# Where GpSimd makes the sums of Wf in a two-layer graph kernel

## The chip, the cores and the metric

One core of one Trainium2 chip runs the kernel. The metric is the device time of a launch in microseconds (us); the time before is the median of three runs. TensorE is PE in the profile, its weight loads are PEld, VectorE is DVE, ScalarE is ACT, GpSimd is POOL, and SP is the engine whose queue issues the DMAs.

## The reference, cut to what matters

The input is `x`, 128 graphs of 64 nodes with 768 features, and `adj`, a mask of 64 x 64 for each graph. Both layers have the form `x = layernorm(x + layer(x, adj))`. Layer 0 is a graph attention with 12 heads, a gate and an ELU. Layer 1, in which the change lies, is a masked attention with six heads of 128:

```
q, k, v = heads(x @ Wq + bq), heads(x @ Wk + bk), heads(x @ Wv + bv)
scores  = einsum('bhqd,bhkd->bhqk', q, k) / sqrt(128)
probs   = softmax(scores + (0 where adj, else -9e15))
ctx     = einsum('bhqk,bhkd->bhqd', probs, v)
x       = layernorm(x + ctx @ Wf + bf)
```

Everything is float32.

## The kernel before, in words

The 8192 tokens are 64 tiles of 128 rows. A pair is two tiles, a group is two pairs. Phase A computes layer 0 pair by pair, and also the products with Wv, whose results go to `v_d` in DRAM. Phase B computes the rest of layer 1 group by group, 16 groups in all.

**Products by sums.** Phase B's products with Wq, Wk and Wf are done by a scheme that needs 15 block products where the plain way needs 18. The token side is split into 6 blocks and the weight into 9; further operands are sums or differences of blocks. The list `SUMS` has the eleven of the token side (`S` for q and k, `Sc` for the context), the list `WEIGHT_SUMS` the fourteen of a weight. `STEPS` lists the 15 block products, each with its token operand, its weight slot, its accumulator and the outputs that it goes to. Each is one step of a `Stream`: four TensorE matmuls in the profile (L896). Each result is added to its outputs by ACT and DVE (L917, L922, L939).

**Who makes the sums.** `weight15_sum(wb, k, eng, o)` makes sum `k` of the weight in tile `wb` on engine `eng` over the columns `o`. On one line (L167) it makes the sums of Wq and Wk, in two halves of the columns (the first half on DVE, the second on POOL), and those of Wf, whole and all on POOL. In the profile the weights have the name `w` whichever they are; a whole sum is 128x512. The token sums of group 0 are made early on DVE, all later ones on POOL by `sum_of_group` (L285). Group 1's are each due two steps after the step of group 0's last stream that reads the tile they overwrite. The first four of group 0's have tiles of their own, so the same sums of group 1 have no such reader. The sums of the context tiles are `pair_sum` (L878).

**What sets the order.** The program is written in steps. `at(step, f)` puts a piece of work on the list of a step, and `run` goes through the lists in order; each engine gets its instructions in the order in which they are so issued, and runs them in that order. The tile framework adds the waits on semaphores. A step of a product comes ahead of all else on its list. Group `g` begins at step `90 * g`: four streams of 15 steps for q and k, of which the last two belong to the odd heads. The following 30 steps hold the two products with Wf of the group before; in group 0 they are empty of products, so on TensorE group 1's first step (step 90) comes right behind step 59 and the group's last scores (L961).

**The softmax of a group** lies in the steps of the next one. For group 0 it starts at step 95, with four parts (`q`, `i`) four steps apart. For a part it is: maximum (`sm_top`, L979, DVE), subtraction (`sm_sub`, L998, DVE), exponential (`sm_exp`, L1001, ACT) three steps after the maximum, row sum (`sm_total`, L1005, DVE), reciprocal and scaling (`sm_scale`: L1009 on DVE, then L1010 on POOL) seven steps after the maximum, transposes on TensorE (`probs`, L1016) with a copy by ACT (L1022) ten steps after it, and the context matmuls (`context`, L1036) thirteen steps after it. The first transposes thus stand at step 105, on TensorE's queue among the steps of group 1's products.

**The sums of Wf.** The tile `wf` takes the place of the weight Wv, which phase A has used up; its six loads stand at steps 2 to 7 (L156), its first sum at step 8, and POOL's halves of the sums of Wq and Wk at steps 9 to 34. The thirteen other sums of Wf stand at steps 68 to 92, two steps apart. Between them and step 34, POOL has group 1's eleven token sums, at steps 47 to 59; after them comes the first scaling of group 0's softmax, at step 102. The first product with Wf is at step 150.

Of the kernel before, what the change touches and what calls it, by code (L numbers as in the profile page):

```python
# [61 lines left out]
def kernel(  # L62
# [31 lines left out]
    nc = tc.nc  # L94
# [52 lines left out]
    def weight15(i):  # L147
        return wts.tile([P, 7, CH, HALF], F32, name=f"w{i}", tag=f"w{i}").rearrange(
            "p s c o -> p (s c o)"
        )[:, : 15 * 2 * 256].rearrange("p (s c o) -> p s c o", s=15, c=2)  # L150
# [14 lines left out]
    def weight15_sum(wb, k, eng, o=slice(0, 256)):  # L165
        to, a, b, sign = WEIGHT_SUMS[k]
        eng.tensor_tensor(wb[:, to, :, o], wb[:, a, :, o], wb[:, b, :, o], SIGN[sign])  # L167
# [647 lines left out]
    def phase_b(ctx, wq, wk, early_sums):  # L815
# [272 lines left out]
        def at(step, *fs):  # L1088
            events.setdefault(max(step, 0), []).extend(fs)
# [14 lines left out]
        wf = weight15(2)  # L1104
# [7 lines left out]
            for k in range(len(WEIGHT_SUMS)):  # L1112
                at(9 + 12 * n + k, lambda wb=wb, k=k: weight15_sum(wb, k, nc.gpsimd, slice(P, 2 * P)))
        for k in range(1, len(WEIGHT_SUMS)):
            at(66 + 2 * k, lambda k=k: weight15_sum(wf, k, nc.gpsimd))
        for g in range(NG):
            d, o = st[g], N * g
            d["S"] = {} if g else early_sums
# [98 lines left out]
    with tc.manual_schedule():  # L1217
        with ExitStack() as c:
            early = phase_a(c)
        with ExitStack() as c:  # L1220
            phase_b(c, *early)
# [31 lines left out]
```

## The time and the profile before

| | |
|---|---|
| median of three runs | 2874.41 us (2872.54 to 2874.44) |
| the profiled execution's own time | 2871.92 us |
| its span | 2870.1 us |
| granted TensorE clock, mean | 0.997 |
| PE busy | 2823.4 us (98%) |
| PEld busy | 2062.7 us (72%) |
| DVE busy | 1862.2 us (65%) |
| POOL busy | 1546.7 us (54%) |
| ACT busy | 1200.4 us (42%) |
| PE's share of the chain that ended last | 85% |

The span is the part of the profiled execution from its first instruction to its last; the time of an execution is 1.8 us more. All times of single events below are microseconds from the span's start. Phase B's first products start at about 1464 us.

A line of a timeline holds the start, the time taken, the engine, the line in the code, the operation with its output and inputs, the count, and in brackets the idle time before it with what ended it. A row of the view of stretches holds the stretch, its length, the busy time and count of PE, PEld, DVE, ACT and POOL, then the granted TensorE clock (1.00 is full), the share of the DMA engines and GB/s.

### The profile page before, as it was taken

How to read it: one execution, taken by the hardware profiler on the slowest of the kernel's cores; microseconds unless marked ns; L12 is line 12 of the kernel's file. 1: busy time of each engine (PE TensorE's matmuls, PEld its weight loads, DVE VectorE, ACT ScalarE, POOL GpSimd, SP SyncE). 2: the span in 40 equal slices, each digit the busy share in tenths (PEclk: the TensorE clock that was granted, in tenths of full speed). 3: DMA queues.
4: the chain of work that ended last, by engine and by line, in shares of the span. 5: the costliest groups of instructions: out<-in, count | busy, mean ns of one | idle time of the engine just before them, and what ended most of it. 6: DMA issues, size and time to landing. Idle time of an engine off the chain costs nothing.

```text
span 2870.1 us, 50797 instructions
## 1 busy us (share of the span) xinstructions
PE 2823.4 (98%) x18108; PEld 2062.7 (72%) x18108; DVE 1862.2 (65%) x3724; ACT 1200.4 (42%) x3737; POOL 1546.7 (54%) x1653
## 2 busy tenths in 40 slices
PE   8899999999999999999999999999999999999998
PEld 5556666555565665655577888888888888888887
DVE  4887777777877777778664555555555555555556
ACT  4666656566566565665622221222221222211223
POOL 4755555555555565555545545345555446454455
PEclk9999999999999999999999999999999999999999
DMA  5434445445344454453631221212221212211222
GB/s 167 121 113 138 147 125 144 128 134 151 114 140 146 126 144 128 134 149 115 210 134 34 89 74 60 79 58 88 90 70 59 83 57 90 89 64 59 89 83 73
DMA packets 358684, 308.40 MB, mean 107 GB/s; under 512 B 226592, under 2 KB 304160, under 8 KB 358432
## 3 DMA queue, kind: packets, MB, share of 16 engines
q1 hardware_dynamic: 358432, 305.16, 34.7%
q8 instruction: 144, 2.36, 0.3%
q14 instruction: 108, 0.88, 0.1%
HBM read 191.41 MB, written 101.06 MB: 102 GB/s over the span
## 4 chain that ended last, share of the span: by engine, by line
PE 85%; DVE 6%; POOL 3%; DMA 2%; ACT 2%; issue 1%; SPq 1%; DVEq 0%; POOLq 0%; ACTq 0%
PE X L896 42%; PE X L209 36%; PE pb L1036 2%; PE pb L961 2%; PE pa L603 1%; DMA s<-dst_d 1%; PE pa L585 1%; PE pb L1016 1%; DVE z L645 1%; ACT s L548 1%; POOL w L167 1%; ACT s L564 1%; DVE s L555 1%; DVE z L636 1%; DVE w L173 0%
## 5 line engine op out<-in xcount | busy, mean ns | idle before, releaser
L209 PE MATMUL X<-w,S 128*128 128x384 f32 x2304 | 796.1, 490 | 10.6 <-DVE w L173 3.3
L896 PE MATMUL X<-S,w 128*128 128x256 f32 x2752 | 651.3, 382 | 0.0
L209 PEld LDWEIGHTS X<-w,S 128*128 128x128 f32 x2304 | 429.9, 190 | 298.0 <-DVE w L173 5.2
L209 PE MATMUL X<-w,T 128*128 128x384 f32 x1728 | 598.1, 489 | 6.9 <-ACT snap L434 5.0
L896 PEld LDWEIGHTS X<-S,w 128*128 128x128 f32 x2752 | 513.6, 190 | 70.1
L209 PEld LDWEIGHTS X<-w,T 128*128 128x128 f32 x1728 | 325.5, 191 | 233.7 <-ACT snap L434 16.2
L878 POOL TENSOR_TENSOR Sc<-cT 128x256 f32<-128x256 f32 x224 | 162.4, 731 | 404.3 <-PE X L896 401.7
L896 PE MATMUL X<-w,Sc 128*128 128x256 f32 x1408 | 322.5, 381 | 0.9 <-DVE xs L939 0.8
L939 DVE TENSOR_TENSOR xs<-xs,X 128x256 f32<-128x256 f32 x512 | 210.6, 419 | 169.0 <-PE X L896 160.5
L896 PEld LDWEIGHTS X<-w,Sc 128*128 128x128 f32 x1408 | 265.5, 190 | 38.5 <-DVE xs L939 1.6
L564 ACT ACTIVATE s<-s,nmx 128x64 f32<-128x64 f32 x768 | 256.2, 335 | 76.7 <-DVE nmx L559 76.7
L922 DVE TENSOR_TENSOR k<-k,X 128x256 f32<-128x256 f32 x320 | 133.5, 421 | 229.2 <-PE X L896 177.3
L896 PE MATMUL X<-xb,w 128*128 128x256 f32 x1024 | 253.1, 380 | 0.4 <-ACT q L917 0.4
L922 DVE TENSOR_TENSOR q<-q,X 128x256 f32<-128x256 f32 x320 | 133.2, 420 | 179.3 <-PE X L896 146.8
L321 ACT ACTIVATE xs<-xs,shift,rstd 128x768 f32<-128x768 f32 x62 | 63.5, 1024 | 417.5 <-POOL shift L317 409.0
L434 ACT COPY snap<-X 128x384 f32<-128x384 f32 x288 | 135.5, 470 | 229.5 <-PE X L209 227.1
L917 ACT ACTIVATE k<-X,bk_c 128x256 f32<-128x256 f32 x192 | 91.1, 474 | 306.3 <-PE X L896 306.3
L498 POOL TENSOR_TENSOR tmp<-th,wd_bc 128x768 f32<-128x768 f32 x64 | 147.5, 2305 | 130.5 <-ACT th L494 107.6
L896 PEld LDWEIGHTS X<-xb,w 128*128 128x128 f32 x1024 | 193.7, 190 | 26.9 <-ACT q L917 0.8
L917 ACT ACTIVATE q<-X,bq_c 128x256 f32<-128x256 f32 x192 | 91.0, 474 | 275.3 <-PE X L896 275.3
L548 ACT ACTIVATE s<-s,src 128x64 f32<-128x64 f32 x768 | 193.1, 335 | 30.5 <-DMA s<-dst_d 30.5
L312 POOL TENSOR_TENSOR rstd<-rstd,neg_half 128x1 f32<-128x1 f32 x126 | 69.4, 551 | 235.0 <-DVE rstd L311 233.7
(120 smaller groups left out, 4103.5 us busy)
## 6 DMA issues: line engine op xcount, KB each, us to landing
xb<-in_x_dram SPq DMA_DIRECT2D x64, 384.0 KB
s<-dst_d SPq DMA_DIRECT2D x128, 192.0 KB
x_d<-xb SPq DMA_DIRECT2D x64, 384.0 KB
xT_d<-T SPq DMA_DIRECT2D x64, 384.0 KB
v_d<-v SPq DMA_DIRECT2D x128, 192.0 KB
xb<-xT_d SPq DMA_DIRECT2D x32, 768.0 KB
xb<-v_d SPq DMA_DIRECT2D x256, 96.0 KB
xs<-x_d SPq DMA_DIRECT2D x64, 384.0 KB
```

The costliest lines, as they stand in the source:

```text
L209: nc.tensor.matmul(o, self.lhsT(i, c), rhs, start=first and c == 0, stop=last and c == CH - 1, skip_group_check=True,)
L312: nc.gpsimd.tensor_tensor(rstd, rstd, neg_half, ALU.pow)
L321: nc.scalar.activation(r, r, AF.Identity, bias=shift, scale=rstd)
L434: nc.scalar.copy(t, ps)
L498: nc.gpsimd.tensor_tensor(self.tmp, self.th, wd_bc, ALU.mult)
L548: nc.scalar.activation(self.s[:, a], self.s[:, a], AF.Prelu, bias=self.src[:, a : a + 1], alpha=LEAKY_ALPHA,)
L564: nc.scalar.activation(self.s[:, a], self.s[:, a], AF.Exp, bias=self.nmx[:, a : a + 1], accum_out=self.sm[:, a : a + 1],)
L878: nc.gpsimd.tensor_tensor(t, pair_part(d, q, r0), pair_part(d, q, r1), op)
L896: nc.tensor.matmul(ps, self.lhsT(r, slot, c), self.rhs(r, slot, c), start=start and c == 0, stop=stop and c == 1, skip_group_check=True,)
L917: nc.scalar.activation(o[:, b], ps, AF.Identity, bias=bias[:, hd : hd + 1], scale=1.0 if positive else -1.0)
L922: nc.vector.tensor_tensor(o[:, b], o[:, b], ps, ALU.add if positive else ALU.subtract)
L939: nc.vector.tensor_tensor(o, o, ps, ALU.add if positive else ALU.subtract)
```

## The change

The thirteen sums of Wf behind the first get other steps. Numbers 1 to 7 go to steps 36 to 42, behind the halves of Wq and Wk (step 34) and in front of group 1's token sums (step 47). Numbers 8 to 13 go to step 66, behind those token sums (step 59) and in front of the first scaling (step 102). Their order among themselves stays. No other work is moved.

```diff
         for k in range(1, len(WEIGHT_SUMS)):
-            at(66 + 2 * k, lambda k=k: weight15_sum(wf, k, nc.gpsimd))
+
+            at(35 + k if k < 8 else 66, lambda k=k: weight15_sum(wf, k, nc.gpsimd))
```

The empty line that comes with it moves the later lines of the code down by one.

## The prediction

> **What bounds the kernel now.** I read the page's busy shares first: PE is busy for 2823.4 of 2870.1 us, so only PE's gaps, or slow matmuls, can give anything. Then the view of waits for PE from 1464 us, the start of layer 1, to the end:
>
> ```profile
> PE pb L1016 <- POOL s L1010: 6.9, 1, 6.9
> PE X L896 <- DVE xs L939: 0.8, 1, 0.8
> PE X L896 <- ACT q L917: 0.4, 1, 0.4
> ```
>
> There is one real wait (us, times, longest): the first transposes of group 0's softmax (L1016) wait 6.9 us for POOL to scale the probabilities (L1010). The timeline of POOL says why:
>
> ```profile
> 1474.48 22.61 POOL L167 TENSOR_TENSOR w<-w 128x512 f32<-128x512 f32 x29 [20.68 <-DMA w<-in_L_gnn_Wf_dram]
> 1497.05 2.50 POOL L285 TENSOR_TENSOR S<-xb 128x512 f32<-128x512 f32 x2
> 1509.69 1.27 POOL L285 TENSOR_TENSOR S<-xb 128x512 f32<-128x512 f32 x1 [10.14 <-PE X L896]
> 1512.28 2.49 POOL L285 TENSOR_TENSOR S<-xb 128x512 f32<-128x512 f32 x2 [1.32 <-PE X L896]
> ...
> 1521.23 1.28 POOL L285 TENSOR_TENSOR S<-xb,S 128x512 f32<-128x512 f32 x1
> 1522.46 17.54 POOL L167 TENSOR_TENSOR w<-w 128x512 f32<-128x512 f32 x13
> 1539.95 1.62 POOL L1010 TENSOR_TENSOR s<-s,rs 128x384 f32<-128x384 f32 x2
> ```
>
> POOL makes two of group 1's token sums at 1497.05, then idles 10.14 us, because the next one overwrites a tile that group 0's matmuls still read. It finishes the eleven at 1522.5, and only then makes thirteen sums of Wf in one block. The scaling is queued behind that block, though its input was there earlier, as the timeline of DVE shows:
>
> ```profile
> 1532.13 0.18 DVE L1009 RECIPROCAL rs<-sm 128x6 f32<-128x6 f32 x1
> ```
>
> On PE's timeline the wait has a second cost:
>
> ```profile
> 1532.89 1.03 PE L896 MATMUL X<-S,w 128*128 128x256 f32 x4
> 1540.84 0.90 PE L1016 MATMUL pb<-ident,s 128*128 128x128 f32 x3 [6.92 <-POOL s L1010]
> 1541.53 1.91 PE L896 MATMUL X<-S,w 128*128 128x256 f32 x4
> 1543.24 1.50 PE L896 MATMUL X<-xb,w 128*128 128x256 f32 x4
> ```
>
> Four matmuls that take 1.03 us ahead of the gap take 1.91 and 1.50 after it. The view of stretches has the clock (the last three columns are PEclk, DMA share, GB/s):
>
> ```profile
> 1533.90:1540.80 6.90, 0.01 (x1) 0.00 (x0) 1.72 (x3) 0.47 (x1) 6.67 (x7) 0.75 0.00 0
> ...
> 1543.00:1544.00 1.00, 1.00 (x4) 0.82 (x3) 0.00 (x0) 0.52 (x2) 0.00 (x0) 0.50 0.00 0
> 1544.00:1545.00 1.00, 1.00 (x5) 0.81 (x5) 0.16 (x1) 0.37 (x1) 0.00 (x0) 0.91 0.00 0
> ```
>
> The clock is at 0.50 from about the middle of the gap to about 1544.2. What this costs is read against group 1, where the same three transposes and three steps run without a wait. From the chain of waits, group 1:
>
> ```profile
> 1629.41 0.33 PE pb L1016 x3
> 1629.74 2.59 PE X L896 x12
> 1632.33 0.86 PE pb L1036 x48
> ```
>
> In group 1 it is 1632.33 - 1629.41 = 2.92 us from the transposes to the context matmuls (L1036). In group 0 the contexts start at 1545.60 in the same view, 4.76 us after 1540.84. From there both groups keep one pace: 4.84 us from one context to the next.
>
> **What the Trainium skill says.** "TensorE: Matmul & The Clock Gate", Part 1, What's actually happening: after an idle window of about 3.4 us PE falls to half clock, and sustained work of about the same length brings it back. The trace agrees: 0.50, and back some 3.4 us after 1540.84. "SBUF — State Buffer", SBUF: two separate sides: a DVE operation with two SBUF inputs and a GpSimd operation that reads SBUF lock each other out for a whole instruction. The trace agrees: DVE's L998 (inputs s and mx) takes up to 1.54 us beside POOL's sums, against a median of 0.55, while L922, with one input in PSUM, has 418 ns beside a busy POOL (1475 to 1497) and 421 where POOL mostly idles (1497 to 1507).
>
> **The change part by part.** No instruction is added or removed, on POOL or elsewhere. The moved steps issue thirteen POOL sums and no DMA, so SP's queue is as before. Only POOL's order changes.
>
> 1. Seven sums go in front. POOL is free at 1497.05. One sum costs 1.35 us in the block of before (17.54 / 13); its single records are 1.26 to 1.59. Seven give 7 x 1.35 = 9.4 us, bounds 8.8 and 11.1. They read rows of Wf that need no new wait: the first sum of Wf waited for this transfer and started at 1474.48, and the DMA row of the stretch 1464 to 1500 is empty from about 1481. Behind them in the queue, the first two token sums are made from about 1506.5 to 1509.0 and not at 1497.05. Their reader is the first step of group 1 at 1519.83: 10.8 us to spare. The next token sum started at 1509.69, on a PE release that stays; with 9.4 us it starts then too. With 11.1 us it would be 1 us late, and the idle 1.32 us behind it takes that up. So I cost the front at **0**: the 10.14 us of POOL's idle time cover it.
>
> 2. Six go behind, in the place of thirteen. The block starts at 1522.46 as before and its sixth record ends at 1530.4. The scaling is next in the queue and now waits for the reciprocal, done at 1532.31. With 0.15 us from reciprocal to scaling (as for the third scaling, 1549.34 to 1549.49) and its 0.83 us, it ends at 1533.3. PE gets to the transposes at 1533.92. So **PE's wait of 6.92 us goes**, with 0.6 us to spare; group 1 has as much (its first scaling ends at 1628.79, its transposes start at 1629.41).
>
> 3. Without a gap of 6.92 us the clock stays at 1.00: **4.76 - 2.92 = 1.84 us** more.
>
> 4. What is late next: during the gap DVE did 1.72 us of work and ACT 0.47, which now lie beside matmuls. In group 1 the same work does so without a wait, so I take 0, with 1.7 as the upper bound. POOL's second scaling needs the reciprocal of 1535.5, and its transposes come about 4.6 us after the first ones: no wait. The v tiles of the contexts come over SP from 1507 on, for PE's release, long before; the fourth waits for the first context and moves with it.
>
> 5. The first reader of the sums of Wf is the second layer's last product, at 1587.8, which moves to 1579. All are done at 1530.4: 0.
>
> Sum: 6.92 + 1.84 = 8.76 us off the end, since every later wait is tied to PE and moves with it. Against the profiled execution's own time that is 2871.92 - 8.8 = 2863.1. The median of the runs shown is 2.5 us above that execution, so the forecast of a median is 2874.41 - 8.8 = **2865.6 us**, 0.30% less. About 0.2%, 5.7 us, is what a measurement of this kernel can tell from no change.
>
> **The rivals.**
> - *The gap closes only in part* (12%). The scaling is only 0.6 us early: a DVE operation locked out for 1 us more would leave PE a wait of 0.4 us, and if DVE's 1.72 us from the gap come back on the path, 1.7 go. For it: L998 is seen at 1.54 us. Against it: until 1530.4 POOL and DVE run just as before, and afterwards POOL has less to do, so DVE can only gain. The gain would be 6.9 to 8.4 us, 2866 to 2867.5. It is also what is left (6.92, so 2867.5) if the half clock has another cause than the gap.
> - *The wait is replaced by another*, of which this trace shows nothing because the gap hides it (5%): 3 to 6 us come back, leaving 2868.5 to 2871.5.
> - *The front is too long* (4%), which ends slower. The seven sums hold up group 1's token sums, and PE waits for them at 1519.8 and after. The token sum with the least to spare is done at 1518.69 and read at the fourth step, 1519.83 + 3 x 0.863 = 1522.4, so 3.7 us to spare. With POOL's 1.32 us idle, and the 0.7 us between 1509.0 and 1509.69, the front may overrun by about 5.7 us: up to 15.1 us in all, 2.2 us a sum. PE pays all beyond that; the loss exceeds the 8.8 us gained from about 24 us, 3.4 us a sum, and 0.2% over that at 4.2 us a sum. This needs sums two and a half times as long as the longest shown (1.59): 2880 us. Nothing speaks for it but that POOL's sums at this place are not in the trace.
> - *The order on POOL is not what the steps say* (2%), because the sums are placed elsewhere: 2874, no change.
>
> **How the numbers follow.** The full gain has 77%. It and the partial one are over 0.2% (6.9 or more against 5.7), less a few per cent for the scatter of the runs (1.9 us among three): faster 0.86. The replaced wait, the order that isn't changed and that scatter give 0.10 within 0.2%. Slower by over 0.2%: 0.04. For the range: full gain plus DVE's relief and the lower runs, 2874.41 - 8.8 - 3 = 2862.5; at the other end the partial gain and half of the replaced wait, 2869.
>
> **What would show it.** Right, if after shows POOL's sums of Wf as seven ahead of the two early token sums, with an idle time of about 1 us and not 10 ahead of the third; six ahead of L1010, which starts near 1532.4; no PE wait for POOL at L1016; PE's clock at 1.00 through the softmax of group 0; PE's busy time 1.8 us lower. Step 1 is wrong if PE waits for S at group 1's first steps, step 2 if L1016 still waits, step 3 if slow matmuls stay, step 4 if PE waits for DVE, ACT or v between 1534 and 1560. A median above 2869 would refute the forecast.

## The result, and the profile after

| | before | after |
|---|---|---|
| median of six runs each | 2874.10 us (2872.54 to 2879.66) | 2864.93 us (2863.35 to 2867.13) |
| profiled execution, its span | 2870.1 us | 2861.8 us |
| PE busy | 2823.4 us | 2821.6 us |
| granted TensorE clock, mean | 0.997 | 0.998 |

The ratio is 0.9966, with a 95% interval of 0.9954 to 0.9979: 6.0 to 13.2 us less, and 9.2 us between the medians. The forecast was a median of 2865.6 us.

The view of waits of PE from 1464 us to the end, after (us, times, longest):

```profile
PE X L896 <- POOL Sc L878: 0.8, 1, 0.8
PE X L896 <- DVE xs L939: 0.8, 1, 0.8
PE X L896 <- ACT q L917: 0.4, 1, 0.4
```

The wait of 6.9 us for the scaling has gone. At the head is a new one, of 0.8 us, for a sum of the context (`Sc`); the last experiment deals with it. POOL's timeline, after:

```profile
1473.68 31.62 POOL L167 TENSOR_TENSOR w<-w 128x512 f32<-128x512 f32 x36 [20.84 <-DMA w<-in_L_gnn_Wf_dram]
1505.25 2.49 POOL L285 TENSOR_TENSOR S<-xb 128x512 f32<-128x512 f32 x2
1508.71 1.26 POOL L285 TENSOR_TENSOR S<-xb 128x512 f32<-128x512 f32 x1 [0.97 <-PE X L896]
...
1521.47 8.08 POOL L167 TENSOR_TENSOR w<-w 128x512 f32<-128x512 f32 x6
1531.48 0.83 POOL L1010 TENSOR_TENSOR s<-s,rs 128x384 f32<-128x384 f32 x1 [1.93 <-DVE rs L1009]
```

The first row has grown from 29 to 36 sums, from 22.61 to 31.62 us: the seven in front take 9.0 us. POOL's idle time ahead of the third token sum has shrunk from 10.14 to 0.97 us. Behind the token sums are six sums and not thirteen, and now POOL waits 1.93 us for the reciprocal, where the reciprocal's result used to wait for POOL.

PE's timeline, and one row of the view of stretches (the third number from the end is the clock), after:

```profile
1531.91 1.03 PE L896 MATMUL X<-S,w 128*128 128x256 f32 x4
1532.77 0.49 PE L1016 MATMUL pb<-ident,s 128*128 128x128 f32 x3
1533.10 1.03 PE L896 MATMUL X<-S,w 128*128 128x256 f32 x4
1533.97 1.03 PE L896 MATMUL X<-xb,w 128*128 128x256 f32 x4
```

```profile
1533.90:1540.80 6.90, 6.90 (x87) 5.58 (x88) 3.78 (x9) 2.69 (x7) 1.82 (x3) 1.00 0.19 55
```

The transposes follow without a gap, the steps behind them take 1.03 us and not 1.91 and 1.50, and the stretch in which PE stood still is full at a clock of 1.00. The chain of waits, after, gives the comparison with group 1 that the prediction used:

```profile
1532.94 0.33 PE pb L1016 x3
1533.26 2.59 PE X L896 x12
1535.86 0.86 PE pb L1036 x48
```

It is 1535.86 - 1532.94 = 2.92 us from transposes to contexts, as in group 1 of the profile of before.

**A measure that the executions' scatter doesn't reach.** Group 1's first step starts at 1519.83 us in the profile of before and at 1518.86 in that of after; in the ten profiles of this study, 1518.86 to 1522.87. The scatter is there already at the first product of layer 1 (1462.86 to 1466.87 us, both times 4.0 us wide), so it arises ahead of it, in layer 0. I therefore measure two pieces in each profile: the **stretch** from group 1's first step (start of the eight matmuls behind the scores L961) to the first contexts (L1036), where the change acts; and the **rest**, from there to the end of the span.

| kernel | PE's gap at the transposes | stretch | against before | rest | ratio of times, 95% interval |
|---|---|---|---|---|---|
| before | 6.92 | 25.77 | | 1324.50 | |
| after | none | 17.00 | -8.77 | 1325.94 | 0.9966 (0.9954 to 0.9979) |
| three in front | 3.37 | 22.01 | -3.76 | 1325.07 | 0.9988 (0.9982 to 0.9995) |
| one in front | 5.81 | 24.80 | -0.97 | 1324.55 | 1.0000 (0.9992 to 1.0008) |
| all in front | none | 18.54 | -7.23 | 1325.28 | 0.9975 (0.9964 to 0.9986) |
| before, gap filled | 0.88 | 24.14 | -1.63 | 1326.17 | 0.9990 (0.9982 to 0.9998) |
| four in front | 2.03 | 20.93 | -4.84 | 1326.38 | 0.9981 (0.9974 to 0.9989) |
| all behind the softmax | none | 17.00 | -8.77 | 1324.47 | 0.9967 (0.9956 to 0.9979) |
| after, later token sums | none | 17.00 | -8.77 | 1324.11 | 0.9962 (0.9949 to 0.9974) |
| after, once more | none | 17.00 | -8.77 | 1326.43 | 0.9970 (0.9960 to 0.9981) |

Gap, stretch and rest are in us and come from one profiled execution of each kernel; the ratio comes from all runs of it. Each ratio is against the kernel before on the same chip. 0.1% is 2.9 us.

### The profile page after: what moved, and what is told of

It is laid out like the page before. It is cut to its first block, busy times and chain, and to the rows that moved or that the text cites. A ratio compares the mean times of both kernels' runs of the same rounds, so it can differ in the third digit from the quotient of the medians.

```text
span 2861.8 us, 50797 instructions
## 1 busy us (share of the span) xinstructions
PE 2821.6 (99%) x18108; PEld 2061.5 (72%) x18108; DVE 1860.6 (65%) x3724; ACT 1199.5 (42%) x3737; POOL 1545.5 (54%) x1653
## 4 chain that ended last, share of the span: by engine, by line
PE 86%; DVE 6%; DMA 2%; ACT 2%; POOL 1%; issue 1%; SPq 1%; DVEq 0%; POOLq 0%; ACTq 0%
PE X L896 43%; PE X L209 36%; PE pb L1036 2%; PE pb L961 2%; PE pa L603 1%; PE pa L585 1%; DMA s<-dst_d 1%; DVE z L645 1%; ACT s L548 1%; PE pb L1016 1%; DVE z L636 1%; ACT s L564 1%; DVE s L555 1%; DVE xb L646 0%; DVE w L173 0%
```

## The experiments

The theory: the gain is PE's gap of 6.92 us, which came from the sums of Wf queued ahead of the first scaling, plus 1.84 us of half clock behind it. The rivals: the slow matmuls have another cause than the gap; or it is DVE, freed from POOL's sums, that brings the gain. The edits below are shown against the changed kernel, but for the filled gap, which is an edit of the kernel before.

### Three and one in front

```diff
-            at(35 + k if k < 8 else 66, lambda k=k: weight15_sum(wf, k, nc.gpsimd))
+            at(35 + k if k < 4 else 66, lambda k=k: weight15_sum(wf, k, nc.gpsimd))
```

With one in front it is `k < 2`.

> Three sums of Wf in front of group 1's token sums and ten behind. Theory A (the gain is PE's gap plus the matmuls that a gap of over about 3.4 us leaves at half clock): the block behind ends at about 1522.4 + 10 x 1.35 = 1536, PE waits about 3.0 us for the scaling, and the clock stays at 1.00, since the gap is shorter than 3.4 us: 6.92 - 3.0 + 1.84 = 5.8 us under the kernel before. Theory B (the slow matmuls behind the gap have another cause than its length): the gap is 3.0 us, the three steps behind the transposes still take 4.8 us and not 2.9: 3.9 us under the kernel before. Theory C (the gain comes from DVE being freed of POOL's sums, not from the queue): about the full gain, 8 us or more, since the order of POOL and DVE beside each other hardly differs.

> One sum of Wf in front and twelve behind. Theory A: the block behind ends 1.35 us earlier than in the kernel before, PE's gap is about 5.6 us, still long enough for the clock to fall: half clock for some 3 us behind the gap, 1.84 us lost as before, and 1.35 us under the kernel before. If the clock's loss grew with the gap's length and did not come in one piece, the loss would be about 1.5 us and the time 1.7 us under before. Theory C: 8 us or more under before.

With three in front the gap was 3.37 us, with one 5.81: it follows the length of the block ahead of the scaling, as the theory has it, and the DVE rival (8 us or more in both) falls. But the matmuls behind the gap were slow with three as well. PE's timeline, three in front:

```profile
1534.77 1.03 PE L896 MATMUL X<-S,w 128*128 128x256 f32 x4
1539.17 0.90 PE L1016 MATMUL pb<-ident,s 128*128 128x128 f32 x3 [3.37 <-POOL s L1010]
1539.86 1.91 PE L896 MATMUL X<-S,w 128*128 128x256 f32 x4
1541.57 1.30 PE L896 MATMUL X<-xb,w 128*128 128x256 f32 x4
```

Steps of 1.91 and 1.30 us stand behind a gap of 3.37, and in stretches of 0.2 us the clock goes to 0.50 at 1538.7, 2.9 us after the last matmul. The stretch lost 22.01 - 17.00 - 3.37 = 1.64 us beside the gap, against 1.85 in the kernel before, and the kernel came out 3.4 us under before (1.4 to 5.2), where I expected 5.8. Its number alone, 3.9 expected for it, spoke for the rival of another cause. One in front lost 24.80 - 17.00 - 5.81 = 1.99 us beside the gap; 1.0 us was gained in the stretch, and nothing that the runs' times can tell.

### The gap filled with useless matmuls

```diff
+        def keep_busy():
+            pc = psb.tile([P, 2, 2, S], F32, name="pb")
+            for m in range(14):
+                nc.tensor.matmul(
+                    pc.rearrange("p a b c -> p (a b c)"), ident, wq[:, m % 9, 0, :], start=True, stop=True
+                )
+
+        at(105, keep_busy)
```

> The kernel before, with fourteen matmuls of no use (identity by a block of Wq, 128x256, into a PSUM tile that nobody reads) put in front of the first transposes of group 0's softmax, some 6.0 us of PE's work inside its gap of 6.9 us. The scaling comes as late as before. Theory A: the gap is full, the clock stays at 1.00, and the three steps behind the transposes take 2.9 us: 1.84 us under the kernel before. Theory B: they take 4.8 us still, and the time is that of the kernel before.

PE's timeline, gap filled:

```profile
1535.51 6.21 PE L1120 MATMUL pb<-w,ident 128*128 128x256 f32 x28
1542.60 0.55 PE L1016 MATMUL pb<-ident,s 128*128 128x128 f32 x3 [0.88 <-POOL s L1010]
1542.98 1.03 PE L896 MATMUL X<-S,w 128*128 128x256 f32 x4
1543.85 1.03 PE L896 MATMUL X<-xb,w 128*128 128x256 f32 x4
```

The scaling is as late as in the kernel before, PE is kept busy, and the steps behind take 1.03 us. The stretch is 1.63 us shorter, and the kernel is 2.9 us faster than before (0.6 to 5.2), though PE does 6 us of work for nothing. So the slow matmuls come from PE's standing still, and the rival of another cause falls. Behind the 0.88 us that are left of the gap the clock is at 1.00, and yet it is 0.55 + 2.59 = 3.14 us from the transposes to the contexts and not 2.92: a break in PE's work costs some 0.2 us beside its length even at full clock. What three in front had shown wrong was the length of gap that it takes.

### Four in front

```diff
-            at(35 + k if k < 8 else 66, lambda k=k: weight15_sum(wf, k, nc.gpsimd))
+            at(35 + k if k < 5 else 66, lambda k=k: weight15_sum(wf, k, nc.gpsimd))
```

> Four sums of Wf in front of group 1's token sums and nine behind. With three in front PE's gap was 3.37 us, 2.4 with each... so one sum of 1.35 us less leaves a gap of about 2.0 us. From group 1's first step to the first context matmuls it is 25.77 us in the kernel before, 22.01 with three in front, 17.00 in the changed one. If the half clock needs a gap of at least about 2.6 us (the shortest time from the last matmul to the clock's fall that was seen), the stretch is 17.0 + 2.0 = 19.0 us and the time some 6.8 us under before. If any gap of about 2 us does it, the stretch is up to 20.8 us and the time some 5 us under before.

Between one and three in front the gap had fallen by 2.44 us for two sums; here it was 2.03 us, as expected, and it too cost the clock. PE's timeline, and rows of the view of stretches, four in front:

```profile
1533.94 1.03 PE L896 MATMUL X<-S,w 128*128 128x256 f32 x4
1537.00 0.55 PE L1016 MATMUL pb<-ident,s 128*128 128x128 f32 x3 [2.03 <-POOL s L1010]
1537.38 1.60 PE L896 MATMUL X<-S,w 128*128 128x256 f32 x4
1538.78 1.91 PE L896 MATMUL X<-xb,w 128*128 128x256 f32 x4
```

```profile
1537.00:1537.50 0.50, 0.50 (x4) 0.50 (x5) 0.00 (x0) 0.00 (x0) 0.50 (x1) 1.00 0.00 0
1538.00:1541.00 3.00, 3.00 (x9) 2.37 (x8) 0.20 (x1) 0.94 (x3) 0.00 (x0) 0.50 0.00 0
1541.50:1543.00 1.50, 1.50 (x52) 1.15 (x51) 0.45 (x2) 0.47 (x1) 0.00 (x0) 1.00 0.05 11
```

When PE resumes at 1537.00 the clock is still 1.00; it falls behind the gap, within the first resumed step, and stays at 0.50 until about 1541. The stretch lost 20.93 - 17.00 - 2.03 = 1.90 us beside the gap: about as much as with gaps of 3.37 to 6.92 us. The stretch of 20.93 is the second case of the expectation; the kernel came out 5.5 us under before (3.2 to 7.5), which by itself fits both cases.

### All thirteen in front

```diff
-            at(35 + k if k < 8 else 66, lambda k=k: weight15_sum(wf, k, nc.gpsimd))
+            at(min(35 + k, 46), lambda k=k: weight15_sum(wf, k, nc.gpsimd))
```

> All thirteen in front of group 1's token sums, none behind: the rival of the prediction in which the front is too long. The front takes 13 x 1.35 = 17.5 us, 2.4 us more than the 15.1 us that I worked out as free. The queue then gives the eleven token sums one after the other from about 1514.6, the one with the least to spare 1.25 x 8 later, at 1524.6, against its reading at 1522.4. Theory A: PE waits about 2.3 us at group 1's fourth step, under 3.4 us, so no half clock; nothing waits at the first transposes; about 6.4 us under the kernel before, 2.3 over the changed one. If my allowance is wrong because token sums other than the fourth step's bind, PE waits at another step, or not at all (then equal to the changed kernel).

Timelines of POOL, then of PE, all in front:

```profile
1473.73 39.36 POOL L167 TENSOR_TENSOR w<-w 128x512 f32<-128x512 f32 x42 [20.68 <-DMA w<-in_L_gnn_Wf_dram]
1513.05 6.19 POOL L285 TENSOR_TENSOR S<-xb 128x512 f32<-128x512 f32 x5
```

```profile
1523.21 2.86 PE L896 MATMUL X<-S,w 128*128 128x256 f32 x12 [1.28 <-POOL S L285]
```

PE waits where I said, at group 1's fourth step, but 1.28 us and not 2.3: the thirteen took 39.36 - 22.61 = 16.75 us, 1.29 each, not 1.35. The clock stays at 1.00 through this gap and behind it; the three steps behind take 2.86 us, where three such steps in a row take 2.75 in the profile of after. The stretch is 1.54 us longer than after's: the gap and 0.26 us beside it, again the price of a break. So seven are not too many in front, but thirteen are. This is the start of the prediction's rival of too long a front; the kernel is still 7.2 us under before (4.0 to 10.3).

### All behind the softmax

```diff
-            at(35 + k if k < 8 else 66, lambda k=k: weight15_sum(wf, k, nc.gpsimd))
+            at(134, lambda k=k: weight15_sum(wf, k, nc.gpsimd))
```

> All thirteen sums of Wf behind the first pair's context sums (step 134), where POOL idles 22.9 us in the changed kernel, and none in front of the token sums or the scalings. Theory A (only the work queued ahead of the first scaling counts): no wait at the transposes, clock at 1.00, the stretch from group 1's first step to the first contexts 17.0 us, the sums done by about 1570 against their first reader at 1578: the time of the changed kernel, 8 to 9 us under before. Rival (the 10 us of POOL's idle time in front were needed): the sums end too late, PE waits at the first steps with Wf, and the time is over that of the changed kernel by as much as it waits.

POOL's timeline, all behind:

```profile
1532.55 0.83 POOL L1010 TENSOR_TENSOR s<-s,rs 128x384 f32<-128x384 f32 x1 [9.94 <-issue]
...
1553.52 16.86 POOL L167 TENSOR_TENSOR w<-w 128x512 f32<-128x512 f32 x13
```

POOL stands idle 9.94 us ahead of the first scaling (the view names no releaser; DVE's reciprocal had ended 0.14 us earlier, at 1532.41), and the kernel is as fast as after: stretch 17.00, 2864.17 us (2863.16 to 2867.11) against 2865.09 (2864.07 to 2868.12) for the changed kernel on the same chip. Filling POOL's idle time in front brought nothing by itself; what counts is how many sums stand between the token sums and the scaling: none or six leave no gap, nine leave one of 2.03 us.

### The changed kernel again, and later token sums

The first of these has no edit. The second moves the token sums of groups 2 and on:

```diff
-                    t = o - 24 + 2 * k
+                    t = o - 16 + 2 * k
```

> The changed kernel once more, for a second profile and for a comparison on the same chip with the kernel that puts all sums behind the softmax. No wait at the first transposes, clock at 1.00 there, the stretch to the first contexts 17.0 us. The wait of 0.84 us for a context sum in group 2 should be another size or absent, if it comes from the scatter of a transfer's landing and not from the change.

> The changed kernel, with the token sums of groups 2 and on each put eight steps later, so that the first of them no longer stands among the context sums of the second pair. In the changed kernel PE waits 0.84 us at 1595.5 for such a context sum, which stands behind a token sum that waits 1.51 us for its tile's transfer. If that is the cause, PE's waits for context sums go in all groups, and the time is at most about 0.8 us under the changed kernel, too little to be told apart by the runs' times: the profile's waits are what is looked at. If the later token sums come too late for the next group's first steps, PE waits for S there.

In the profile of after, the new wait is this. Timelines of POOL, then of PE:

```profile
1586.59 1.27 POOL L285 TENSOR_TENSOR S<-xb 128x512 f32<-128x512 f32 x1 [1.51 <-DMA xb<-xT_d]
```

```profile
1596.34 2.86 PE L896 MATMUL X<-w,Sc 128*128 128x256 f32 x12 [0.84 <-POOL Sc L878]
```

A token sum of group 2 waits for its tile's transfer and holds up the context sums behind it in POOL's queue, and PE waits for one of them. The first line of PE's waits, changed kernel again:

```profile
PE X L896 <- POOL Sc L878: 1.4, 3, 0.7
```

It is 1.4 us in three waits here, 1.2 with the gap filled, where the order on POOL is that of before, 1.4 with four in front, 0.2 to 0.3 in three others, and not in the view for before or for all behind. The view leaves out the shortest waits: PE's timeline of before has one of 0.14 us for a context sum, at 1865.59. So the wait has another size in every execution, also where the order on POOL is that of before, and the change is not needed for it. With the token sums eight steps later PE's waits are down to

```profile
PE X L896 <- DVE xs L939: 0.8, 1, 0.8
PE X L896 <- ACT q L917: 0.4, 1, 0.4
```

and the rest is the shortest of the ten, 1324.11 us. Its five runs (2861.92 to 2863.10 us, median 2862.94) all lie under the seven of the changed kernel on the same chip. The medians are 2.2 us apart and the rests 1.8 and 2.3, more than the 0.8 us that I allowed. Set beside the profile of after, the 1.8 us are found: context sums stopped PE there at 1596.34, 1856.95 and 2551.12 us, for 0.84, 0.14 and 0.02 us, and each break cost 0.26 to 0.27 us beside its length, 1.8 in all. None of the three is left. Its ratio to before is 0.9962 (0.9949 to 0.9974); that it is faster than the changed kernel too rests on five runs against seven, and on these waits in one profile of each.

## Why the prediction was right, point by point

- **Step 1, seven in front at no cost: right.** They took 9.0 us (9.4 said), the idle time left was 0.97 us ("about 1"), and the third token sum still waits for PE. All in front showed where the cover ends: 16.75 us in front left a wait of 1.28, so some 15.5 us are free, and I had said 15.1.
- **Step 2, the gap goes: right.** Against group 1's first step the scaling ended at 13.45 us; the prediction's times give 1533.3 - 1519.83 = 13.5. PE got to the transposes 0.6 us later, as said.
- **Step 3, 1.84 us of clock: right in size, with the cause shown, but not all of it is the clock's.** Transposes to contexts went from 4.76 to 2.92 us, and the filled gap gave 1.63 us of this back without moving the scaling; the other 0.2 us are the price of the break itself. What was wrong is a thing the forecast did not rest on: the Trainium skill's page "TensorE: Matmul & The Clock Gate", Part 1, What's actually happening, puts the half clock after an idle window of about 3.4 us, and in the profile of before the clock did fall 3.4 us after the last matmul. I took that, in the expectation for three in front, as the shortest gap that costs anything. A gap of 2.03 us cost 1.90 us, so here the measurement decides. The partial rival, priced with a clock that stays up, would have been dearer than I said had its gap been 2 us.
- **Step 4, nothing late next: right at the softmax.** DVE kept up: the L998 of the third part took 0.55 us where it had taken 1.54 beside POOL's sums. The sentence that "every later wait is tied to PE" was too strong: POOL's wait for group 2's tile is tied to a transfer's landing. It cost PE 0.84 us in this profile, and 0.26 us beside that for the break. A second break at 2551.12 us, with only 0.02 us of standing still, cost 0.29 in all. Together these are 1.39 of the 1.44 us by which the rest is longer than in before's profile.
- **Step 5: right.** The last of the sums of Wf ended at 1529.55; the first product with them started at 1578.05.
- **The sum**: 8.76 said, 8.77 in the stretch. The times moved 9.2 us by the medians, with an interval of 6.0 to 13.2 that cannot tell the two apart. That the forecast of the median came within 0.7 us is in part luck, since the runs of the changed kernel alone lie 3.8 us apart.

## What to carry to other kernels

An engine with half its time free can still hold the bound engine up: look at what stands in its queue ahead of the one instruction that is waited for, and move whatever is due later to behind it. A gap of TensorE has two prices, its length and the slow matmuls behind it; here the second was about the same for a gap of 2 us as for one of 7, so halving the gap (3.37 us for 6.92) brought 3.76 of the 8.77 us. Where runs scatter by nearly as much as the change, measure from a fixed event just ahead of it to one just behind it.

## What I had not expected of the hardware

- The clock fell for gaps of 2.03, 3.37, 5.81 and 6.92 us, and not for 0.88 and 1.28; between 1.28 and 2.03 it is open. Each is one profiled execution, so whether a gap of 2 us always costs it is not shown. The loss beside the gap was 1.90, 1.64, 1.99 and 1.85 us. In stretches of 0.2 us the fall came 2.6 to 3.4 us after the last matmul, and the half clock lasted some 3.4 us with the two short gaps and 6.8 us, gap included, with the two long ones.
- The loss can be worked out from this. PE ran at half clock for 3.41, 2.94, 3.64 and 3.34 us of work behind the gaps, and loses half of that time. With 0.22 us for the break this gives an estimate of 1.92, 1.69, 2.04 and 1.89 us, each within 0.05 us of the loss measured.
- At full clock, too, a break in PE's work cost more than its length: 0.22 us at the transposes and 0.26 to 0.27 us at the products, for breaks of 0.02 to 1.28 us. Why is not shown.
- The ten profiled executions reach group 1's first step between 1518.86 and 1522.87 us, though TensorE's work up to there is the same in all of them: 4 us of scatter arise in the first layer.
